# Deformable convolution: the last tile of tokens taken three taps at a time

## The chip, the cores and the metric

The kernel runs on one core of one Trainium2 chip. The metric is the device time of one execution in microseconds (us); lower is better. Times given as a median are of executions without the profiler; the profile is of one further execution.

## The reference

Four layers follow one another on an image batch of 4 x 56 x 56 x 128 floats: a window-attention block, a state-space block, a deformable convolution and another window-attention block, each as `x = x + layer(group_norm(x))`. The change lies in the third layer alone, which the reference computes like this:

```python
offsets = conv(x, offset_w) + offset_b            # 9 taps x (dy, dx) for every pixel
py, px = row + ky + dy, col + kx + dx
y0, x0 = floor(py), floor(px); wy, wx = py - y0, px - x0
val = gather(y0, x0) * (1 - wy) * (1 - wx) + gather(y0, x0 + 1) * (1 - wy) * wx \
    + gather(y0 + 1, x0) * wy * (1 - wx) + gather(y0 + 1, x0 + 1) * wy * wx
out = einsum('bhwkc,kcf->bhwf', val, kernel.reshape(9, C, F)) + bias
...
x = x + L2(group_norm(x))
```

So for every pixel and each of 9 taps, four neighbours of 128 channels are fetched from places that depend on the data, weighted and added, and the nine results are multiplied by a 128 x 128 matrix each and summed.

## The kernel before, in words

The batch of four images is walked one image at a time (`run`), and each image goes through the four layers. `x` holds an image with channels on the 128 partitions and 3136 tokens along the free side. Inside `deform` the kernel writes its own order (`manual_schedule`): each engine executes its instructions in the order in which the Python text issues them, and waits are inserted where data or a buffer demand it.

The tokens are cut in two ways. A **tile** is 112 tokens (`QB`), and there are 28 of them (`NTB`), numbered `t` = 0 to 27. A **chunk** is four tiles, 448 tokens (`CH`), and there are seven (`NCK`), numbered `c` = 0 to 6. Nine taps (`KK`) are handled in three groups of three. Five helpers make up the loop:

- `gather(t)` issues nine indirect DMAs on GpSimd (L1265), one for each tap. They fill the tile `g`, 112 tokens x 9 taps x 512 values; there are four such buffers.
- `weigh(t)` works on VectorE (DVE), three instructions for each group of taps: L1366 multiplies the two far neighbours by their weights into PSUM (`pa`), L1367 multiplies the near ones in place, L1368 adds the two.
- `turn(t)` transposes on TensorE (PE): six instructions for each group of taps (L1379), which also add the two remaining halves, into a PSUM tile `pvt`. ScalarE (ACT) copies each `pvt` into the chunk's tile `vt` (L1380).
- `product(c, i)` multiplies taps 3i to 3i+2 of a whole chunk by the kernel's matrices and accumulates them in the PSUM tile `pdo` (L1387). There is one `pdo` buffer. Each of the three matrix products of a call shows in the trace as two MATMUL records.
- `add(c)` adds `pdo` and the bias to `x` on DVE (L1391), and takes the chunk's statistics for the next group norm (`stats`, L117).

The loop over tiles runs one chunk behind itself: while the tiles 0, 1 and 2 of chunk c are turned, the three products of chunk c-1 are issued, and at tile 3 of chunk c comes `add(c - 1)`. For the last tile, t = 27, this means that DVE gets `weigh(27)` and then `add(5)`, and PE gets `turn(27)`. After the loop come `product(6, 0)`, `product(6, 1)`, `product(6, 2)` and `add(6)`. Then the next layer, `swin("L3")`, begins with its group norm (`gn_mv` L128, `gn_pm` L130), which needs the statistics of all seven chunks, and with the normalized windows `xw` (L235). GpSimd also clears buffers for it, beginning with `ks` (L336).

Of the kernel before, what the change touches and what calls it, by code (L numbers as in the profile page):

```python
# [23 lines left out]
NCK = L // CH  # L24
# [12 lines left out]
NTB = L // QB  # L37
# [12 lines left out]
KK = 9  # L50
# [28 lines left out]
class _Net:  # L79
# [1169 lines left out]
    def deform(self, b, x):  # L1249
# [7 lines left out]
        with tc.tile_pool(name="df", bufs=1) as s1, tc.tile_pool(name="df_ps", bufs=1, space=PSUM) as s1x, tc.manual_schedule():  # L1257
            idx = s1.tile([QB, n2], I32, tag="idx", name="idx")
            patch = {}

            def gather(t):
                patch[t] = s1.tile([QB, KK, 4 * P], F32, tag="g", name="g", bufs=4)
                for k in range(KK):

                    nc.gpsimd.indirect_dma_start(  # L1265
                        out=patch[t][:, k], out_offset=None, in_=tab[:, :],
                        in_offset=bass.IndirectOffsetOnAxis(ap=idx[:, t * KK + k : t * KK + k + 1], axis=0),
                    )
# [4 lines left out]
            with tc.tile_pool(name="dc", bufs=1) as sb, tc.tile_pool(name="dc_ps", bufs=6, space=PSUM) as ps:  # L1273
# [7 lines left out]
                for c in range(NCK):  # L1281
# [3 lines left out]
                    for i in range(nq):  # L1285
                        t = c * nq + i
# [21 lines left out]
                for g in range(2):  # L1308
                    n = min(4, NCK - 4 * g)
                    pf = bank("pf")  # L1310
                    for k in range(KK):
                        ky, kx = k // 3, k % 3
                        for j in range(n):
                            c = 4 * g + j
# [40 lines left out]
            with tc.tile_pool(name="dg", bufs=2) as sb, tc.tile_pool(name="dg_ps", bufs=2, space=PSUM) as ps:  # L1355
                turned, made = {}, {}

                def weigh(t):

                    g = patch[t].rearrange("q k (s c) -> q k s c", s=4)  # L1360
                    wv = wts[2 * t // NTB][:, t % (NTB // 2) * KK : (t % (NTB // 2) + 1) * KK, :, None].to_broadcast([QB, KK, 4, P])
                    for k in range(0, KK, 3):
                        ks = slice(k, k + 3)
                        pa = ps.tile([P, 2, 512], F32, tag="pa", name="pa", bufs=1)
                        far = pa[:QB].rearrange("q a b -> q (a b)")[:, : 6 * P].rearrange("q (k s c) -> q k s c", k=3, s=2)
                        nc.vector.tensor_tensor(far, g[:, ks, 2:, :], wv[:, ks, 2:, :], ALU.mult)  # L1366
                        nc.vector.tensor_tensor(g[:, ks, :2, :], g[:, ks, :2, :], wv[:, ks, :2, :], ALU.mult)  # L1367
                        nc.vector.tensor_tensor(g[:, ks, :2, :], g[:, ks, :2, :], far, ALU.add)  # L1368

                def turn(t):  # L1370
                    c, i = divmod(t, nq)
                    if i == 0:
                        turned[c] = sb.tile([P, KK, CH], F32, tag="vt", name="vt")
                    g = patch.pop(t)
                    for k in range(0, KK, 3):
                        pt = ps.tile([P, 3, QB], F32, tag="tr", name="pvt", bufs=3)
                        for m in range(3):
                            for s in range(2):
                                nc.tensor.matmul(pt[:, m, :], lhsT=g[:, k + m, s * P : (s + 1) * P], rhs=self.ident[:QB, :QB], start=(s == 0), stop=(s == 1), is_transpose=True)  # L1379
                        nc.scalar.copy(turned[c][:, k : k + 3, i * QB : (i + 1) * QB], pt)  # L1380

                def product(c, i):

                    if i == 0:
                        made[c] = ps.tile([P, 512], F32, tag="y", name="pdo", bufs=1)
                    for k in range(3 * i, 3 * i + 3):
                        nc.tensor.matmul(made[c][:, :CH], lhsT=w["kernel"][:, k * P : (k + 1) * P], rhs=turned[c][:, k, :], start=(k == 0), stop=(k == KK - 1))  # L1387

                def add(c):
                    cols = slice(c * CH, (c + 1) * CH)  # L1390
                    nc.vector.scalar_tensor_tensor(x[:, cols], made.pop(c)[:, :CH], w["bias"], x[:, cols], ALU.add, ALU.add)  # L1391
                    self.stats(x, c)


                for t in range(NTB):
                    c, i = divmod(t, nq)
                    if t >= 4:
                        gather(t)
                    weigh(t)
                    if c >= 1 and i == 3:  # L1400
                        add(c - 1)
                    turn(t)
                    if c >= 1 and i < 3:
                        product(c - 1, i)
                for i in range(3):
                    product(NCK - 1, i)
                add(NCK - 1)

    def finish(self, b, x, cols):
# [108 lines left out]
```

## Time and profile before

| | |
|---|---|
| median of 3 executions | 13293.08 us (13291.37 to 13294.18) |
| profiled execution | 13095.61 us |
| its span, first to last instruction | 13093.7 us |
| mean granted TensorE clock | 0.943 of full speed |
| busy share of PE, DVE, ACT, POOL | 89%, 74%, 58%, 76% |
| busy time of L1265 (gathers), all images | 940.8 us, 1008 instructions |
| busy time of L1379 (transposes), all images | 366.7 us, 2016 instructions |

The profiled execution is 197.47 us shorter than the median of the others, and its span leaves 1.91 us of its own time outside. Shares of busy time are averages over four layers in which different engines are the busiest. The trace is one execution; in it a stretch of time is named in us from the start of the span. The four images go through the deformable layer near 2112 to 2434, 5380 to 5704, 8650 to 8970 and 11914 to 12241 us.

### The profile page before, as it was taken

The numbers are of one execution on the slowest core, as the hardware profiler recorded it, in microseconds if no ns is written. First come the engines' busy times: TensorE is split into PE (matmuls) and PEld (weight loads), VectorE is DVE, ScalarE is ACT, GpSimd is POOL, SyncE is SP. The second block draws the span as 40 slices with busy tenths as digits, with TensorE's granted clock in tenths as the row PEclk, the third lists the DMA queues.
The fourth block names the chain that finished last, engine by engine and source line by source line (L and its number), as shares of the span: only waits on it lengthen the run. The fifth ranks groups of instructions, "written<-read, shape, count | busy, mean of one in ns | idle before, by whom it ended". The sixth has DMA issues, their size and how long they took to land. (4 is left out here: it accounts for less than half of the span.)

```text
span 13093.7 us, 216642 instructions
## 1 busy us (share of the span) xinstructions
PE 11654.7 (89%) x84932; PEld 7362.6 (56%) x84932; DVE 9728.0 (74%) x11883; ACT 7560.0 (58%) x19097; POOL 9942.8 (76%) x6852
## 2 busy tenths in 40 slices
PE   8989996799898999679989899967999989996799
PEld 4438884444543888444454388844445438884444
DVE  6659996665665999666566599966656659996665
ACT  5567772356556777235655677723565567772356
POOL 4949995498494999549759499954974949995497
PEclk9999997899999999789999999978999999997899
DMA  1000003200000000420000000042000000004200
GB/s 59 1 14 4 5 4 114 74 1 9 3 1 14 4 5 4 116 72 1 10 2 1 14 5 5 4 120 68 1 11 1 1 14 5 5 4 121 66 1 6
DMA packets 155644, 317.88 MB, mean 24 GB/s; under 512 B 19660, under 2 KB 89344, under 8 KB 154496
## 3 DMA queue, kind: packets, MB, share of 16 engines
q0 software_dynamic: 80640, 231.28, 6.1%
q1 hardware_dynamic: 73696, 71.21, 1.8%
q8 instruction: 672, 11.01, 0.3%
q14 instruction: 348, 2.85, 0.1%
q10 hardware_dynamic: 288, 1.53, 0.0%
HBM read 256.04 MB, written 47.90 MB: 23 GB/s over the span
## 5 line engine op out<-in xcount | busy, mean ns | idle before, releaser
L569 POOL TENSOR_TENSOR es<-es,e 128x896 f32<-128x896 f32 x2016 | 4159.3, 2090 | 133.1 <-ACT e L563 75.1
L363 DVE TENSOR_REDUCE mx<-pm 128x1 f32<-128x512 f32 (+1 forms) x4928 | 3057.9, 671 | 1401.5 <-PE pm L362 787.3
L563 ACT ACTIVATE e<-pst 128x448 f32<-128x448 f32 (+1 forms) x5600 | 2678.4, 544 | 1886.8 <-PE pst L561 1351.4
L1083 DVE TENSOR_TENSOR_SCAN hs<-da,dbu 128x928 f32<-128x928 f32 x1792 | 3633.1, 2070 | 52.2 <-ACT dbu L1076 30.0
L1092 POOL TENSOR_TENSOR hs<-hs,cb 128x896 f32<-128x896 f32 x1792 | 3473.8, 1951 | 25.0 <-ACT carry L1087 20.3
L362 PE MATMUL pm<-ks,qs 32*128 32x512 f32 (+1 forms) x9856 | 2906.1, 633 | 13.3 <-DVE nm L384 7.8
L561 PE MATMUL pst<-qs,ks 32*128 32x448 f32 x11200 | 2684.0, 547 | 0.0
L1101 PE MATMUL yt<-w_C,hs 128*116 128x128 f32 x14336 | 1865.1, 273 | 1.1 <-POOL hs L1092 1.1
L556 PE MATMUL pst<-nm,sel 32*128 32x448 f32 x5600 | 1637.1, 614 | 0.0
L1101 PEld LDWEIGHTS yt<-w_C,hs 128*116 128x116 f32 x14336 | 1571.2, 135 | 2.1 <-POOL hs L1092 2.1
L1065 PE MATMUL dbu<-dgb,ut 112*128 112x224 f32 x7168 | 1258.6, 298 | 268.0 <-DVE hs L1083 267.8
L585 PE MATMUL po<-e,va 128*32 128x448 f32 (+1 forms) x11200 | 1350.8, 551 | 0.0
L362 PEld LDWEIGHTS pm<-ks,qs 32*128 32x128 f32 x9856 | 923.4, 185 | 746.2 <-DVE mx L363 619.3
L1065 PEld LDWEIGHTS dbu<-dgb,ut 112*128 112x128 f32 x7168 | 946.2, 192 | 533.1 <-DVE hs L1083 523.3
L1265 POOL DMA_INDIRECT g<-tab,idx x1008 | 940.8, 933 | 393.6 <-issue 283.1
L1019 ACT ACTIVATE da<-dl,A 128x112 f32<-128x112 f32 x3584 | 1193.9, 382 | 0.1
L561 PEld LDWEIGHTS pst<-qs,ks 32*128 32x128 f32 x11200 | 1096.8, 185 | 100.9 <-issue 12.7
L556 PEld LDWEIGHTS pst<-nm,sel 32*128 32x128 f32 x5600 | 569.9, 184 | 739.9 <-DVE mx L363 387.1
L1379 PE MATMUL pvt<-w_C,g 112*128 112x112 f32 x2016 | 366.7, 338 | 623.4 <-issue 520.4
L1380 ACT COPY vt<-pvt 128x336 f32<-128x336 f32 x336 | 147.2, 438 | 1126.5 <-PE pvt L1379 1126.5
L288 POOL TENSOR_TENSOR pz<-s,m 64x784 f32<-64x784 f32 x128 | 191.8, 1498 | 751.9 <-DVE m L285 520.0
L1087 ACT COPY carry<-hs 128x32 f32<-128x32 f32 x1792 | 397.2, 222 | 624.0 <-DVE hs L1083 615.9
(237 smaller groups left out, 15945.1 us busy)
## 6 DMA issues: line engine op xcount, KB each, us to landing
g<-tab,idx POOLq DMA_INDIRECT x1008, 3.4
tab<-zero SPq DMA_DIRECT2D x4, 3364.0 KB
dl_d<-dl SPq DMA_DIRECT2D x28, 448.0 KB
dl<-dl_d SPq DMA_DIRECT2D x56, 224.0 KB
tab<-gt SPq DMA_DIRECT2D x16, 448.0 KB
out_dram<-x SPq DMA_DIRECT2D x28, 224.0 KB
tab<-gt SPq DMA_DIRECT2D x16, 336.0 KB
x<-in_x_dram SPq DMA_DIRECT2D x21, 224.0 KB
```

Source lines behind the costliest of these rows:

```text
L362: nc.tensor.matmul(pm[:, :m], lhsT=qs[head(h), q.start : q.start + P], rhs=ks[head(h), keys], start=True, stop=True)
L363: nc.vector.tensor_reduce(mx[:, home[i][1], h, kc : kc + 1], pm[:, :m], AX.X, ALU.max)
L556: nc.tensor.matmul(t[:, :CH], lhsT=self.sel[head(h), :], rhs=nm[head(h), part(qc)], start=True, stop=False)
L561: nc.tensor.matmul(t[:, :CH], lhsT=ks[head(h), k * KB : (k + 1) * KB], rhs=qs[head(h), part(qc)], start=False, stop=True)
L563: nc.scalar.activation(e[:nk, j, :], t[:nk, :CH], AF.Exp, scale=SCALE)
L569: nc.gpsimd.tensor_tensor(s, es[g - 1, p][:nk] if k == 1 else s, e[:nk], ALU.add)
L585: nc.tensor.matmul(m["po"][head(h), :CH], lhsT=va[:nk, k, head(h)], rhs=src(h)[:nk], start=(k == 0), stop=(k == NKB - 1))
L1019: nc.scalar.activation(m["da"][:, :, n, 2:], dl(), AF.Exp, scale=A[:, j, n : n + 1])
L1065: nc.tensor.matmul(pu[:, 8 * h : 8 * h + 8, 2 + tb * TB : 2 + (tb + 1) * TB], lhsT=made[g]["ut", 2 * r + tb][:, d, :], rhs=made["r", g // ...
L1083: nc.vector.tensor_tensor_scan(flat(pairs[u // 2][:, d % 2]), flat(made[g]["da"][:, r]), flat(banks.pop(u)), 0.0, ALU.mult, ALU.add)
L1092: nc.gpsimd.tensor_tensor(hs, hs, made["r", g // 2]["cb"][:, :, r * HW : (r + 1) * HW], ALU.mult)
L1101: nc.tensor.matmul(sums[q][:YR, e * P : (e + 1) * P], lhsT=hs[:, n, :], rhs=self.ident, start=(n == 0), stop=(n == NST // 2 - 1), is_trans ...
```

## The change

`weigh` and `turn` take an argument that says which groups of taps they handle. The loop over tiles issues everything for t = 0 to 26 as before, and for t = 27 only the gathers. What is left comes after the loop: first `add(5)`, then for each group of three taps `weigh`, `turn` and, from the second group on, the product of the group before. `product(6, 2)` and `add(6)` are last. The tiles in `patch` are no longer dropped from the dictionary when they are turned.

```diff
-                def weigh(t):
+                def weigh(t, taps=range(0, KK, 3)):
...
-                    for k in range(0, KK, 3):
+                    for k in taps:
...
-                def turn(t):
+                def turn(t, taps=range(0, KK, 3)):
...
-                    g = patch.pop(t)
-                    for k in range(0, KK, 3):
+                    g = patch[t]
+                    for k in taps:
...
-                    weigh(t)
-                    if c >= 1 and i == 3:
-                        add(c - 1)
-                    turn(t)
-                    if c >= 1 and i < 3:
-                        product(c - 1, i)
+                    if t < NTB - 1:
+                        weigh(t)
+                        if c >= 1 and i == 3:
+                            add(c - 1)
+                        turn(t)
+                        if c >= 1 and i < 3:
+                            product(c - 1, i)
+
+                add(NCK - 2)
                 for i in range(3):
-                    product(NCK - 1, i)
+                    weigh(NTB - 1, (3 * i,))
+                    turn(NTB - 1, (3 * i,))
+                    if i >= 1:
+                        product(NCK - 1, i - 1)
+                product(NCK - 1, 2)
                 add(NCK - 1)
```

In the changed program as built, the order of instructions differs at four places, one for each image. On PE the end of the layer was L1379 x18, L1387 x9, and is now L1379 x12, L1387 x3, L1379 x6, L1387 x6. On DVE the pair L1391, L117 of chunk 5 moves ahead of the nine instructions of `weigh(27)`. ACT, GpSimd and the DMA queues have the same instructions in the same order, and every tile has the same address.

## The prediction

> **What bounds the kernel now.** I began with the page. PE is the busiest engine overall, but the change touches one layer, and there the groups point elsewhere: the gathers on GpSimd, while PE's transposes stand idle longer than they work.
>
> ```profile
> PE 11654.7 (89%) x84932; PEld 7362.6 (56%) x84932; DVE 9728.0 (74%) x11883; ACT 7560.0 (58%) x19097; POOL 9942.8 (76%) x6852
> ...
> L1265 POOL DMA_INDIRECT g<-tab,idx x1008 | 940.8, 933 | 393.6 <-issue 283.1
> L1379 PE MATMUL pvt<-w_C,g 112*128 112x112 f32 x2016 | 366.7, 338 | 623.4 <-issue 520.4
> ```
>
> A gather starts every 1.24 us (0.93 busy, 0.30 idle in the timeline), three taps take 3.7 us, and DVE's three instructions for them 2.80 us: DVE waits for the DMA before nearly every group. So in the loop the gathers set the pace; only what follows the last one (issued at 12224.42 in the fourth image) can be shortened. Next I read the timeline of DVE at that end:
>
> ```profile
> 12220.67 0.96 DVE L1366 TENSOR_TENSOR pa<-g,wt 112x768 f32<-112x768 f32 x1 [1.14 <-DMA g<-tab,idx]
> 12221.54 0.95 DVE L1367 TENSOR_TENSOR g<-g,wt 112x768 f32<-112x768 f32 x1
> 12222.52 0.95 DVE L1368 TENSOR_TENSOR g<-g,pa 112x768 f32<-112x768 f32 x1
> 12224.29 0.96 DVE L1366 TENSOR_TENSOR pa<-g,wt 112x768 f32<-112x768 f32 x1 [0.81 <-DMA g<-tab,idx]
> ...
> 12229.72 0.95 DVE L1368 TENSOR_TENSOR g<-g,pa 112x768 f32<-112x768 f32 x1
> 12230.59 0.68 DVE L1391 SCALAR_TENSOR_TENSOR x<-pdo,w_L,x 128x448 f32<-128x448 f32 x1
> 12231.30 0.63 DVE L117 BATCH_NORM_STATS2 gn_st<-x 128x6 f32<-128x448 f32 x1
> ```
>
> The three groups of tile 27 start at 12220.67, 12224.29 and 12227.87 and end at 12230.67. The add of chunk 5, behind them, waits for nothing. The chain of waits shows who is last:
>
> ```profile
> 12220.54 3.82 PE pdo L1387 x6
> 12224.36 0.59 PE pvt L1379 x6
> ...
> 12227.20 1.37 PE pvt L1379 x6
> ...
> 12230.77 1.35 PE pvt L1379 x6
> 12232.13 7.68 PE pdo L1387 x18
> 12239.81 0.02 issue
> 12239.83 0.69 DVE x L1391
> ```
>
> Two facts decide my forecast. The path is the last group's weighing, its transposes, then all 18 MATMUL records of chunk 6, 7.68 us, with DVE idle 7.90 us and the next layer behind it. And the product of chunk 5 (first line) ends at 12224.36, **after** weigh(27) has begun at 12220.67.
>
> Last, the granted clock in stretches (columns: stretch, length, PE busy, clock, DMA share, GB/s):
>
> ```profile
> 12226.00:12227.00 1.00, 0.00 (x0) 0.98 0.71 211
> 12227.00:12228.00 1.00, 0.80 (x5) 0.50 0.06 21
> 12230.40:12233.80 3.40, 3.03 (x9) 0.50 0.00 0
> 12233.80:12237.20 3.40, 3.40 (x10) 1.00 0.00 0
> ```
>
> **What the skill says, and whether the trace agrees.** The Trainium skill, page "TensorE: Matmul & The Clock Gate", section "Part 1: The HAM clock gate", says PE's clock is halved until a free-running window of about 3.4 us has been busy. The trace agrees: only 0.5 and 1.0 occur, and switches fall on a grid of 3.41 us (about 12226.98, 12230.40, 12233.81). A window with PE busy for 1.3 to 1.5 us of 3.4 stayed at half speed (as 12226.98 to 12230.40); one with 3.0 us brought full speed. The threshold between is unseen. The same page, section "Architectural detail", says DVE's queue is strict FIFO and PE pulls only weight loads forward. The timelines agree: no DVE instruction here overtakes a waiting one. So whatever stands behind a waiting add waits too.
>
> **The change part by part**, for the fourth image.
>
> *Add and statistics of chunk 5, moved ahead of weigh(27).* Two DVE instructions, on no queue but DVE's. Before, they cost nothing: they ran under the last transposes. Now the add reaches the head of DVE at about 12219.6, when weigh(26) ends, and needs pdo, finished at 12224.36. That is a **new wait of 4.8 us**, and the nine instructions of weigh(27) stand behind it, though the DMA for the first six taps lands by 12224.29. The add starts at 12224.38, the statistics 0.71 later, the next L1366 0.54 after them (12186.75 to 12187.29 in the timeline): 12225.63, instead of 12220.67. From here all data has landed in time, so groups follow without gaps, 0.87 + 0.98 + 0.87 = 2.72 us apart: 12228.35 and 12231.07. The last ends 2.80 later, at **12233.87 instead of 12230.67**. The DMA wait that hid under the old order is regained, which is why 4.96 us late at the start becomes 3.20 at the end.
>
> *Transposes and products, re-ordered.* Nothing is added to PE. The second group's transposes can start 0.10 after its L1368, at 12231.25. product(6, 0) follows 1.15 later, as before (12230.77 to 12231.92), at 12232.40; its ACT copy is long done. Six records cost 0.745 each at half clock or 0.375 at full clock (starts of the weight loads). The third group's transposes now stand behind this product; their data is ready at 12233.97, so PE, not DVE, is late by then. They take 0.6 at full clock, and the remaining 12 records 12 x 0.375 = 4.5, plus 0.2 for the end of the last one (so calibrated, the old 18 records give 12239.8). ACT's copy of the last group, 0.45 us, lies under product(6, 1).
>
> What is unknown is when full clock comes. The window 12230.40 to 12233.81 would be busy 2.56 of 3.41 us, between the shares seen. (a) If that suffices: 1.41 us of half clock (1.9 records) and 4.1 x 0.375 bring 12235.35; + 0.6 + 4.5 + 0.2 = 12240.65, **0.85 later** than 12239.81. (b) If not, 6 x 0.745 ends at 12236.87, transposes at 12237.6, end at 12242.3, **2.5 later**. I take the middle, 1.6, and keep both.
>
> *Waits.* PE's built list loses one wait on DVE before the products, and the last transposes wait for an earlier group of PE's own instead of an ACT copy. Nearest row: a semaphore event on PE's queue took 0.051 us. So between a gain of 0.05 and a loss of 0.2 (one drained product); I take 0. *patch no longer emptied*: no instruction or address changes; 0.
>
> *The other images* have the same shape: in all four, pdo of chunk 5 ends 6.1 to 6.3 us before the last weighing ends, and the final product ends 15.4 to 15.5 us after pdo of chunk 5. Sum: 4 x 1.6 = 6.4, bounds 4 x 0.85 = 3.4 and 4 x 2.5 = 10, with waits 3.2 to 10.8. Against its own 13095.61 the profiled execution would read 13102. The unprofiled median stood 197 us higher, and I add the same difference to it: 13293.1 + 6 = **13299 us**.
>
> **The rivals.**
>
> *The overlap pays.* Were DVE not held, product(6, 0) would start at 12228.35, run at half clock to 12230.40 and end at 12231.6; transposes and two products bring 12236.9, 2.9 us sooner, 11.6 in all: 13281.5. For it: PE idles 2.26 and 2.22 us between these transposes, and DVE has slack. Against it: the order of adds and weighings in DVE's list and the 12224.36 above. It needs the product of chunk 5 over by 12221, which its transposes (12219.63) do not allow.
>
> *Clock stays low, clearly slower.* The end becomes several bursts with gaps. If neither window after 12230.40 brings full clock, the end is 12232.40 + 4.47 + 1.15 + 8.94 + 0.2 = 12247.2, 7.3 us later, 29 in all: 13322, slower by 0.22%. It decides if PE still shows 0.50 beyond 12237.2. For it: the window before is only 40% busy. Against it: from 12231.25 on PE has no gap[...].
>
> *Clearly faster* needs 6.6 us an image. The last six records plus transposes cannot start before the old 12230.77, so 12230.77 + 0.6 + 2.25 + 0.2 = 12233.8, six us less, is a floor that even a perfect overlap does not pass.
>
> **How the numbers follow.** A measurement of this kernel tells about 0.2%, 26.6 us, from no change. Late add, 3 to 11 us slower: 0.80. Overlap pays: 0.10. Clock stays low: 0.06, on the border, counted as slower. Something unforeseen: 0.04. So faster 0.03, same 0.90, slower 0.07. The range takes the two likeliest cases, 13281.5 to 13304, with some way toward the third: 13281 to 13312.
>
> **What would show it right or wrong.** In the profile after: L1391 of chunk 5 waits 4 to 5 us for PE pdo in each image (before, it waits only for chunk 6: 31.9 us over 4 times); the three L1366 behind it follow 2.72 us apart with no DMA wait; the last weighing ends 3.2 us later; DVE's wait for the last pdo stays between 6.8 and 8.4 us (7.9 before); the end moves by 0.8 to 2.5 us. If L1391 of chunk 5 shows no wait, the step that carries the forecast is wrong.

## The result, and the profile after

The changed kernel took **13338.04 us** (13320.64 to 13348.71, 8 executions) against 13295.36 us (13290.79 to 13303.87, 8 executions) of the kernel before: a ratio of 1.003, interval 1.002 to 1.0039, or 42.7 us more. Repeated on three chips, the difference was 36.9, 37.0 and 34.7 us. The forecast was 6 us.

The page after, three rows of its groups. It shows one of the eight timed executions (13342.97 us). The columns are line, engine, operation, tiles, count; then busy time and mean ns of one; then the idle time just before them and what ended most of it.

```profile
L1265 POOL DMA_INDIRECT g<-tab,idx x1008 | 943.8, 936 | 565.7 <-issue 288.6
...
L1379 PE MATMUL pvt<-w_C,g 112*128 112x112 f32 x2016 | 343.0, 337 | 930.9 <-issue 544.7
...
L1380 ACT COPY vt<-pvt 128x336 f32<-128x336 f32 x336 | 141.2, 441 | 1362.3 <-remote 885.8
```

The gathers work as long as before (943.8 us, 940.8 before), but stand idle 172 us longer than in the profile that the prediction used. And ACT's copies now wait mostly for something that the trace can't name ("remote"). Before, their 1126.5 us of idle time were all put down to PE's transposes:

```profile
L1380 ACT COPY vt<-pvt 128x336 f32<-128x336 f32 x336 | 147.2, 438 | 1126.5 <-PE pvt L1379 1126.5
```

The change does not touch either of them, so this already says that the two profiles differ in more than the change.

DVE's timeline of the kernel after, end of the fourth image (columns: start, length, engine, line, operation; in brackets the idle time and what ended it):

```profile
12460.24 0.95 DVE L1368 TENSOR_TENSOR g<-g,pa 112x768 f32<-112x768 f32 x1
12470.86 0.68 DVE L1391 SCALAR_TENSOR_TENSOR x<-pdo,w_L,x 128x448 f32<-128x448 f32 x1 [9.66 <-PE pdo L1387]
12471.58 0.63 DVE L117 BATCH_NORM_STATS2 gn_st<-x 128x6 f32<-128x448 f32 x1
12472.12 0.94 DVE L1366 TENSOR_TENSOR pa<-g,wt 112x768 f32<-112x768 f32 x1
...
12479.64 0.95 DVE L1368 TENSOR_TENSOR g<-g,pa 112x768 f32<-112x768 f32 x1
12487.80 0.68 DVE L1391 SCALAR_TENSOR_TENSOR x<-pdo,w_L,x 128x448 f32<-128x448 f32 x1 [7.21 <-PE pdo L1387]
```

The new wait is there, and longer than the 4.8 us of the forecast. The add of chunk 5 holds DVE for 9.66 us, and the whole of `weigh(27)` comes after it. The chain of waits of the same stretch shows what follows:

```profile
12468.55 2.27 PE pdo L1387 x6
12470.82 4.19 issue
12475.01 1.37 PE pvt L1379 x6
...
12479.21 3.46 PE pdo L1387 x6
12482.66 0.58 PE pvt L1379 x6
12483.24 4.54 PE pdo L1387 x12
12487.78 0.03 issue
12487.80 0.69 DVE x L1391
```

Chunk 5's product ends at 12470.82, and PE then stands still for 4.19 us while DVE adds and weighs. From the end of chunk 5's product to that of the final product (below: **the tail**) it is 16.9 us here.

One plain fact is needed to read all this. The profile of the kernel before, 13095.61 us, and the timed executions, 13291 to 13304 us, show one program in two conditions, and in these runs each chip showed only one of them. One of the chips used later ran the same kernel in 13099.90 us (13091.41 to 13120.36, 11 executions), four others in 13281 to 13292. The change was measured in the second condition, and forecast from the first. On which chip the profile of the kernel before was taken is not on record.

### The profile page after: what moved, and what is told of

Read it like the earlier page. It is cut to its first block, busy times and chain, and to the rows that moved or that the text cites. A ratio compares the mean times of both kernels' runs of the same rounds, so it can differ in the third digit from the quotient of the medians.

```text
span 13340.9 us, 216634 instructions
## 1 busy us (share of the span) xinstructions
PE 11587.4 (87%) x84932; PEld 7345.5 (55%) x84932; DVE 9743.9 (73%) x11883; ACT 7558.2 (57%) x19097; POOL 9948.8 (75%) x6852
## 5 line engine op out<-in xcount | busy, mean ns | idle before, releaser
L1265 POOL DMA_INDIRECT g<-tab,idx x1008 | 943.8, 936 | 565.7 <-issue 288.6
L1379 PE MATMUL pvt<-w_C,g 112*128 112x112 f32 x2016 | 343.0, 337 | 930.9 <-issue 544.7
L1379 PEld LDWEIGHTS pvt<-w_C,g 112*128 112x128 f32 x2016 | 288.7, 187 | 1015.2 <-issue 621.6
```

## The experiments

The tables here are worked out from the traces. "Late groups" are groups of six transposes whose ACT copy starts over 3 us after their last record ends (of 336). The trace models when a transpose ends, so a late copy can mean a late signal or a transpose that in truth ended late; no run tells the two apart, and "late signals" below stands for both. "Tail" is the mean over the four images. "Gathers" is from the first to the last of an image, and "layer" the sum of the four deformable layers from the group norm of one layer to that of the next.

### The kernel before once more, and the order of DVE alone

`same` is the kernel before, unedited.

> The kernel before, unchanged, for a trace in the condition of the timed executions (13291 to 13304 us, where the profile shown had 13096). Theory A (the difference is made at the end of each image's deformable layer by the add that is held up): the trace has the loop over tiles at the pace of the gathers, as in the profile shown, and the 200 us lie elsewhere. Theory B (the loop over tiles itself runs slower in timed executions, in both kernels, and the change makes it more so): the stretch from the layer's group norm to the next layer's, 351 us in the profile shown and 403 to 409 us in the profile of the changed kernel, measures about 395 us here. Time: ratio 1.000 in both.

`addfirst` moves only the add:

```diff
+                    if t == NTB - 1:
+                        add(c - 1)
                     weigh(t)
-                    if c >= 1 and i == 3:
+                    if c >= 1 and i == 3 and t < NTB - 1:
                         add(c - 1)
```

> The kernel before with one part of the change alone: add(5) ahead of weigh(27); products still after all transposes. Theory A: the last weighing ends 3.2 us later and all of it is on the path, so 4 x 3.2 = 13 us slower, about 13308. Theory B: the hold matters more, because TensorE is further behind in timed executions; as slow as the changed kernel, 13335 or more.

`lateadd` has the changed kernel's order for weighing, turning and multiplying, but puts the add back behind two of the three groups of weighing (the edit is one of the changed kernel):

```diff
-                add(NCK - 2)
                 for i in range(3):
                     weigh(NTB - 1, (3 * i,))
                     turn(NTB - 1, (3 * i,))
+                    if i == 1:
+                        add(NCK - 2)
                     if i >= 1:
                         product(NCK - 1, i - 1)
```

> The changed kernel with add(5) issued after the second group's weighing and transposes, just ahead of product(6, 0). Theory A: DVE is held later and less, the overlap pays: 2.9 us an image sooner than before, about 13284. Theory B, in the form that the hold of the whole weighing costs the 42 us: near before, within 10 us of 13295. Theory C (the order of the products or the number of instructions, not the add, makes the loop slower): still 13335.

`after_again` is the changed kernel, unedited.

> The changed kernel once more beside the others on the same chip: 13338, that is 42 us slower than before, if the difference is one of the kernels; nearer to 13300 if it was one of the chip at that time.

All four ran on one chip, beside the kernel before at 13281.67 us; the table's first and last row are other executions.

| kernel | us | ratio, interval | late groups | gathers, us | tail, us | layer, us |
|---|---|---|---|---|---|---|
| profile that the prediction used | 13095.61 | | 0 | 311 | 15.4 | 1404.8 |
| same | 13282.00 | 0.9999 (0.999 to 1.0007) | 144 | 350 to 354 | 8.5 | 1586.2 |
| addfirst | 13323.26 | 1.0029 (1.0019 to 1.0038) | 149 | 350 to 354 | 19.8 | 1633.7 |
| lateadd | 13284.39 | 1.0003 (0.9995 to 1.0012) | 145 | 350 to 354 | 9.5 | 1591.4 |
| after_again | 13318.60 | 1.0026 (1.0015 to 1.0037) | 145 | 354 | 17.4 | 1609.2 |
| after (first result) | 13338.04 | 1.003 (1.002 to 1.0039) | 145 | 350 to 356 | 17.2 | 1624.0 |

This settles two things. First, the place of the add makes the loss: moved alone, it costs 41.6 us, and with it moved back, the three-taps order costs 2.7 us (5.9 and 7.8 us on two further chips, below), no difference that these runs can tell. Second, the tail gives the size. All that stands ahead of the end of chunk 5's product is the same in these kernels, so a longer tail is time lost. Four images of 17.2 - 8.5 = 8.7 us make 35 us, four of 19.8 - 8.5 = 11.3 make 45, and four of 9.5 - 8.5 = 1.0 make 4. The totals moved by 37 to 43, 42 and 3 us. The layer's sum in a single trace scatters more: against `same` it is 37.8 and 23.0 us longer in the two traces of the changed kernel, 47.5 in `addfirst` and 5.2 in `lateadd`.

The tail is so short in `same` because DVE is early and PE late. DVE's timeline of `same`, fourth image:

```profile
12417.54 0.95 DVE L1368 TENSOR_TENSOR g<-g,pa 112x768 f32<-112x768 f32 x1
12419.15 0.96 DVE L1366 TENSOR_TENSOR pa<-g,wt 112x768 f32<-112x768 f32 x1 [0.66 <-DMA g<-tab,idx]
...
12428.40 0.95 DVE L1368 TENSOR_TENSOR g<-g,pa 112x768 f32<-112x768 f32 x1
12431.12 0.69 DVE L1391 SCALAR_TENSOR_TENSOR x<-pdo,w_L,x 128x448 f32<-128x448 f32 x1 [1.77 <-PE pdo L1387]
12431.84 0.63 DVE L117 BATCH_NORM_STATS2 gn_st<-x 128x6 f32<-128x448 f32 x1
12439.63 0.68 DVE L1391 SCALAR_TENSOR_TENSOR x<-pdo,w_L,x 128x448 f32<-128x448 f32 x1 [7.16 <-PE pdo L1387]
```

`weigh(27)` follows `weigh(26)` after 0.66 us and ends before chunk 5's product does. The add waits for PE even here, 1.77 us, with nothing behind it that matters. After that product only PE's own work is left: 18 transposes and the product of chunk 6, 8.5 us. So the weighing is hidden under PE's backlog, in all four images of this trace. Moving the add ahead of it takes that cover away, as `addfirst` shows in DVE's timeline:

```profile
12468.64 0.96 DVE L1368 TENSOR_TENSOR g<-g,pa 112x768 f32<-112x768 f32 x1
12480.78 0.68 DVE L1391 SCALAR_TENSOR_TENSOR x<-pdo,w_L,x 128x448 f32<-128x448 f32 x1 [11.18 <-PE pdo L1387]
...
12489.56 0.95 DVE L1368 TENSOR_TENSOR g<-g,pa 112x768 f32<-112x768 f32 x1
12499.88 0.69 DVE L1391 SCALAR_TENSOR_TENSOR x<-pdo,w_L,x 128x448 f32<-128x448 f32 x1 [9.37 <-PE pdo L1387]
```

The wait is 11.18 us, and all of 8.5 us of weighing lies between it and PE's transposes. In the changed kernel the tail is 2.6 us shorter than here, since it turns and multiplies the first groups while DVE weighs the later ones: the overlap that the change sets up does exist, and gives back about a quarter (2.6 of 11.3 us) of what the add costs. With the add in third place (`lateadd`, the same view) two of the three groups are weighed before the wait, and only the last group is behind it:

```profile
12423.91 0.95 DVE L1368 TENSOR_TENSOR g<-g,pa 112x768 f32<-112x768 f32 x1
12433.81 0.68 DVE L1391 SCALAR_TENSOR_TENSOR x<-pdo,w_L,x 128x448 f32<-128x448 f32 x1 [8.94 <-PE pdo L1387]
...
12435.07 0.94 DVE L1366 TENSOR_TENSOR pa<-g,wt 112x768 f32<-112x768 f32 x1
...
12443.29 0.68 DVE L1391 SCALAR_TENSOR_TENSOR x<-pdo,w_L,x 128x448 f32<-128x448 f32 x1 [5.43 <-PE pdo L1387]
```

A wait of 8.94 us costs nearly nothing here: when it ends, two groups lie weighed, and PE turns them and begins on chunk 6 while DVE adds and weighs the third. It is what stands behind the waiting instruction that counts, not the wait.

### Why PE has a backlog: its signals and the gathers

The trace of `same` around a gap in the fourth image, PE, ACT and GpSimd in turn:

```profile
12384.32 1.31 PE L1379 MATMUL pvt<-w_C,g 112*128 112x112 f32 x12
12385.86 0.79 PE L1379 MATMUL pvt<-w_C,g 112*128 112x112 f32 x6 [0.23 <-issue]
12408.28 1.38 PE L1379 MATMUL pvt<-w_C,g 112*128 112x112 f32 x6 [21.63 <-issue]
```

```profile
12407.79 0.44 ACT L1380 COPY vt<-pvt 128x336 f32<-128x336 f32 x1 [21.98 <-issue]
12412.75 1.12 ACT L1380 COPY vt<-pvt 128x336 f32<-128x336 f32 x3 [4.52 <-remote]
```

```profile
12406.88 0.93 POOL L1265 DMA_INDIRECT g<-tab,idx  x1 [0.30 <-issue]
12413.06 0.93 POOL L1265 DMA_INDIRECT g<-tab,idx  x1 [5.25 <-remote]
```

These are three groups of transposes, the first ended at 12385.06 and the last at 12386.65. ACT, idle since 12385.81, copies the first at 12407.79, 22.7 us later, and the last at 12413.08, 26.4 us later. PE has three `pvt` buffers and cannot go on without the copies. The signals come through in bursts, here when the gathers pause. In the profile that the prediction used, ACT follows most groups after 0.04 us and every one within 0.2 us.

The trace's own record of semaphores (the counters by which engines and DMAs signal each other) differs in the same way. The gathers should leave 16128 updates in it, 16 for each gather. The profile that the prediction used, `paced64` and `paced128` below have all of them, and the four traces with slow gathers 98 to 99%. All the others have 14 to 34%, `same` 3056. Whether the missing updates were merged or only not recorded can't be told. But it means that "remote" and "issue" name no cause in these traces.

The transfers themselves are not slower: one packet of the gathers takes 163 ns on average in `same` and 158 ns in the profile that the prediction used.

Three questions followed. Is it the bytes of the gathers, their rate, or the few `pvt` buffers?

`half_before` and `half_after` fetch half the bytes, without and with the change. They leave out the second row of neighbours and use the first in its place, so they do not compute the layer:

```diff
-                        out=patch[t][:, k], out_offset=None, in_=tab[:, :],
+                        out=patch[t][:, k, : 2 * P], out_offset=None, in_=tab[:, :],
...
-                        nc.vector.tensor_tensor(far, g[:, ks, 2:, :], wv[:, ks, 2:, :], ALU.mult)
+                        nc.vector.tensor_tensor(far, g[:, ks, :2, :], wv[:, ks, 2:, :], ALU.mult)
```

> The order before, but each gather fetches only the first 256 of 512 values of a token (1 KB instead of 2 KB), and weigh takes both pairs of neighbours from them: the second row of neighbours is left out, all instructions keep their number and size. Theory B1 (TensorE's completion signals come late because of the bytes that the gathers move): the signals of the 336 transposed groups that reach ACT over 3 us late fall from 144 to under 30, the gathers of an image take about 311 us instead of 354, and about 170 us are saved, 13110. Theory B2 (it is the number of gathers or of their descriptors, not the bytes): 144 late groups remain, time within 30 us of 13282.

> The same cut of the gathers in the changed kernel's order. If the late signals are gone, the arithmetic of the prediction holds again: 3 to 11 us slower than half_before. If they remain: 35 to 45 us slower than half_before.

`slow_before` and `slow_after` have GpSimd clear 512 values on each partition after every gather, `paced64` and `paced128` (of the kernel before) 64 and 128 values:

```diff
+            idle = s1.tile([P, 512], F32, tag="idle", name="idle")
...
+                    nc.gpsimd.memset(idle, 0.0)
```

> The order before, all bytes gathered, with a memset of 128x512 on GpSimd after each gather (0.53 us busy in the profile of the kernel before), so that gathers come about every 1.8 to 2.1 us instead of 1.24. Theory B1 and B2 (too many gathers or bytes at a time hold the signals back): late groups fall under 30, the gathers of an image take 450 to 530 us, total slower by 400 to 700 us. If the lateness has nothing to do with the gathers' rate, 100 or more late groups remain.

> The same in the changed kernel's order. TensorE then has time to finish product(5, 2) before the last group of tile 26 is weighed or soon after; by the prediction's arithmetic the hold of DVE costs at most 4.8 us an image and the end moves by under 2.5: within 10 us of slow_before. If the hold costs about 10 us an image whatever TensorE's lag: 40 us slower than slow_before.

> The order before, all bytes gathered, with a short memset (128x64) on GpSimd after each gather: a gather about every 1.3 us (1.24 without it, 1.65 with the memset of 128x512, where no completion signal was late; without it the pauses bring the mean to 1.41). If the signals are late because gathers come faster than something can serve, and 1.3 us is already slow enough: no late groups of 336, the gathers of an image take 320 to 335 us, the layer ends as in the first profile, and 80 to 140 us are saved: 13140 to 13200. If the limit lies between 1.3 and 1.41: late groups remain, 100 or more, and the time is within 20 us of 13281.

> The same with a memset of 128x128: a gather about every 1.35 us. With the signals in time: no late groups, 335 to 350 us for the gathers of an image, 20 to 80 us saved, 13200 to 13260. If they are still late: within 20 us of 13281 or slower.

The last two met the chip on which the kernel before takes 13099.90 us and no group of theirs was late, so `paced64` was run again on another, beside the changed kernel and `lateadd`:

> A gather every 1.27 us. If the kernel before takes about 13100 here: 45 us slower, as measured. If about 13280 and the signals are late because gathers come faster than 1.27 us: no late groups, gathers of an image 319 us instead of 354, about 13145 and so 130 us faster. If 1.27 us is still too fast: 100 or more late groups and within 20 us of before.

> The changed kernel on the chip of this call. If the kernel before takes about 13100 here (TensorE's signals in time, as in the first profile): the prediction's arithmetic, 3 to 11 us slower, and the end of the layer 0.8 to 2.5 us later an image after product(5, 2). If it takes about 13280 (signals late): 35 to 45 us slower again.

> add(5) just ahead of product(6, 0). If the kernel before takes about 13100 here: DVE is not held behind product(5, 2), the overlap pays, 2.9 us an image, 12 us faster (the rival of the prediction, never seen with signals in time). If about 13280: within 10 us of before, as measured.

`tr5` gives PE five `pvt` buffers instead of three, and moves the tile `wt` out of PSUM to make room:

```diff
-            wps = s1x.tile([P, 2, 512], F32, tag="wt", name="wt")
+            wps = s1.tile([P, 2, 512], F32, tag="wt", name="wt")
...
-                        pt = ps.tile([P, 3, QB], F32, tag="tr", name="pvt", bufs=3)
+                        pt = ps.tile([P, 3, QB], F32, tag="tr", name="pvt", bufs=5)
```

> The order before, with five pvt buffers instead of three (the bilinear weights wt move from PSUM to SBUF to make room). If ACT's late copies cost time because TensorE runs out of pvt buffers: the pauses of the gathers shrink and 20 us or more are saved where the signals are late. If the late signals alone set the pace: within 15 us of before. Where they are in time: within 15 us of before.

> The changed kernel on the chip of this call. If the kernel before takes about 13100 here (signals in time): the prediction's arithmetic, 3 to 11 us slower, product(6, 2) ending 16.3 to 17.9 us after product(5, 2) instead of 15.4. If about 13280 (signals late): 35 to 45 us slower, and 17.2 us instead of 8.5.

> add(5) just ahead of product(6, 0). With the signals in time: the overlap pays, product(6, 2) ends about 12.5 us after product(5, 2) instead of 15.4, 12 us faster. With the signals late: 9.5 us instead of 8.5, within 10 us of before.

Lines are grouped by the chip that they share.

| kernel | us | kernel before beside it | ratio, interval | late groups | gathers, us | layer, us |
|---|---|---|---|---|---|---|
| half_before | 13292.71 | 13281.20 | 1.0008 (1.0001 to 1.0014) | 148 | 353 to 356 | 1602.1 |
| half_after | 13323.66 | | 1.0037 (1.0023 to 1.005) | 145 | 355 to 356 | 1620.6 |
| slow_before | 13504.89 | | 1.017 (1.0156 to 1.0184) | 0 | 413 | 1815.5 |
| slow_after | 13521.44 | | 1.0183 (1.0169 to 1.0196) | 0 | 413 | 1812.5 |
| paced64 | 13145.13 | 13099.90 | 1.0031 (1.0019 to 1.0042) | 0 | 319 | 1442.1 |
| paced128 | 13194.70 | | 1.0069 (1.0055 to 1.0083) | 0 | 334 | 1500.5 |
| paced64_c | 13298.02 | 13291.55 | 1.0005 (0.9997 to 1.0013) | 160 | 356 to 359 | 1603.4 |
| after_c | 13328.50 | | 1.003 (1.0017 to 1.0042) | 147 | 355 to 356 | 1618.6 |
| lateadd_c | 13297.43 | | 1.0 (0.9992 to 1.0009) | 155 | 356 | 1589.3 |
| tr5 | 13287.43 | 13285.25 | 1.0002 (0.9993 to 1.001) | 119 | 354 to 355 | 1581.8 |
| after_d | 13319.91 | | 1.0025 (1.0016 to 1.0033) | 146 | 354 | 1611.3 |
| lateadd_d | 13293.07 | | 1.0003 (0.9994 to 1.0011) | 146 | 350 to 354 | 1593.1 |

*Bytes are not it*: half of them left the late groups and the gathers' 355 us as they were, and the change still cost 31 us. The tail says the same: 10.1 us on average in `half_before` and 18.0 in `half_after`, four times the difference being 32 us. *The rate matters*: one gather every 1.65 us (`slow_before`) leaves no group late, on a chip where gathers issued every 1.24 us, with pauses, leave about 145. It is not the clearing as such, since `paced64_c` clears too, if less, and still has 160 late groups. The page of `slow_before2`, the same kernel on a further chip, puts nearly all of ACT's idle time down to PE again:

```profile
L1382 ACT COPY vt<-pvt 128x336 f32<-128x336 f32 x336 | 147.2, 438 | 1537.3 <-PE pvt L1381 1504.2
```

*The buffers are not it either*: with five of them, the layer takes the same time, but GpSimd's timeline (fourth image) looks different:

```profile
12396.40 1.40 POOL L1265 DMA_INDIRECT g<-tab,idx  x1 [0.31 <-issue]
12398.11 0.93 POOL L1265 DMA_INDIRECT g<-tab,idx  x1 [0.30 <-issue]
12399.35 0.93 POOL L1265 DMA_INDIRECT g<-tab,idx  x1 [0.30 <-issue]
12400.59 1.48 POOL L1265 DMA_INDIRECT g<-tab,idx  x1 [0.31 <-issue]
```

The pauses of some 6 us are mostly gone, and instead every third gather takes 1.3 to 1.5 us in place of 0.93. PE's backlog at the end is mostly gone too: the add of chunk 5 waits for nothing in three images, and there the tail is 15.8 to 15.9 us. As chunk 5's product ends earlier, the total is the same, so tails compare only kernels that do the same ahead of it. The changed order with five buffers was not run. The sum is the same: in `same`, `half_before`, `paced64_c` and `tr5` an image's 251 intervals between gathers take 350 to 359 us, 1.39 to 1.43 us each, however the delay is spread. The Trainium skill, page "Perfetto Trace Analysis", section "DMA Instruction — SWDGE (GPSIMD)", says that the profile ends such a DMA when its descriptors are written and not when its data have moved, and that more can be generated than the descriptor buffer holds. The 1.40 us beside 0.93 us fit a full buffer, though no run shows the buffer itself. So I read the 1.4 us as the pace that these chips keep for these gathers, against 1.24 us or less in the profile that the prediction used. That reading is drawn from these kernels alone; no run changed the pace itself, and what makes PE's signals late near it was not found.

The pair with slow gathers is the nearest to what the prediction described, because there DVE waits for data again. Its difference, 16.6 us, was larger than the layer's own (-3.0 us), so it was repeated:

> The paced order before once more: 13505 if the chip has late signals with the kernel before; no late groups; the end of the layer's last product 15.8 us after the last gather, as measured.

> The paced changed order once more. Its layer measured 3 us less than slow_before's in the traces, its total 17 us more. If the 17 us are the execution's or the clock's (the next layer's time varies by several us with TensorE's clock): within 10 us of slow_before2. If they come with the order: 12 to 20 us slower again, and again in the layer after.

Now it was 8.0 us (13514.15, 13499.2 to 13525.84; 13522.13, 13511.64 to 13528.93), with the layer's sum at 1814.7 and 1814.8 us. DVE's timeline of `slow_after2`, fourth image:

```profile
12651.03 0.95 DVE L1370 TENSOR_TENSOR g<-g,pa 112x768 f32<-112x768 f32 x1
12657.66 0.68 DVE L1393 SCALAR_TENSOR_TENSOR x<-pdo,w_L,x 128x448 f32<-128x448 f32 x1 [5.68 <-PE pdo L1389]
12658.38 0.63 DVE L117 BATCH_NORM_STATS2 gn_st<-x 128x6 f32<-128x448 f32 x1
12658.92 0.94 DVE L1368 TENSOR_TENSOR pa<-g,wt 112x768 f32<-112x768 f32 x1
...
12675.86 0.68 DVE L1393 SCALAR_TENSOR_TENSOR x<-pdo,w_L,x 128x448 f32<-128x448 f32 x1 [8.47 <-PE pdo L1389]
```

With signals in time the add holds DVE for 5.68 us, near the 4.8 us of the forecast, and the DMA waits behind it are regained. These waits are longer here, some 2 us for a group where the forecast had about 1. So the layer's last product ends sooner, 14.9 us after the start of the last gather instead of 15.5, where the forecast had it 0.85 to 2.5 us later. The mechanism is the forecast one, but the balance is not the same, so this pair does not measure the forecast itself.

What the whole kernel loses there, 8 to 17 us, lies outside the layer. In the traced executions, which differ by 14.3 and 29.7 us, the layer behind takes 11.1 and 21.1 us more. In the second image of `slow_after2` it takes 4.4 us more than in `slow_before2`, all of it in its first 170 us; near its start PE's clock stays halved for 13.7 us instead of 6.8. Why the clock comes up later there was not found.

## Why the prediction was wrong

*Right in mechanism.* The add of chunk 5 waits in every image, and `weigh(27)` stands behind it. The Trainium skill, page "TensorE: Matmul & The Clock Gate", section "Architectural detail", says that DVE's queue is strict FIFO, and the trace agrees: L1366 comes only after the held add and its statistics, at 12472.12. The groups behind it start without a DMA wait, 2.83 us apart (2.72 forecast). DVE waits 7.0 to 8.0 us for the last `pdo` (6.8 to 8.4 forecast). The last twelve records take 4.54 us (4.5 forecast at full clock), so the clock does come up: the rival in which it stays low is out.

*Right for the state after.* By the prediction's own numbers the tail after would be 12240.65 - 12224.36 = 16.3 us in case (a), and 12242.3 - 12224.36 = 17.9 us in case (b). It measured 17.2 us on average, single images 16.8 to 17.8. This is no luck: once the add has waited, all data has landed, and the work that follows is the same however late the add was. One reading was wrong, though with little effect: "The threshold between is unseen". Cut into windows of 3.41 us, the trace of the kernel before has 49 at half clock in which PE is busy for 50 to 80%, and each is followed by another at half clock. That speaks for case (b). Nor is a busy window enough: of 141 at half clock with PE busy for over 95%, 13 are followed by half clock.

*Wrong for the state before.* The failed step is the one sentence "The unprofiled median stood 197 us higher, and I add the same difference to it". It treats the 197 us as a constant beside the change. Nearly all of them lie in the changed layer: it takes 1586.2 - 1404.8 = 181 us more in the trace of `same`, of 192 us between the two traced executions, while each of the other three layers agrees within 6.3 us over all images. There the gathers and PE keep other times. So the tail before is 8.5 us and not 15.4, and the term of the sum is 8.7 us an image instead of 1.6. What made the loss small, a DMA wait to be regained on the path and the weighing as the last thing there, holds where PE keeps up, as in the profiled execution. In `same` DVE still waits for the DMA before the groups of tile 27 (0.66, 0.88 and 0.91 us in the fourth image), but PE's backlog hides them. The wait itself, sized at 4.8 us from when DVE and PE reach the add, was 7.9 to 15.1 us.

*The rivals.* "The overlap pays" named the condition on which it fails, chunk 5's product not over when `weigh(26)` is, and it failed on that: the product ended 7.9 to 15.1 us after it. "Clock stays low, clearly slower" came nearest to the size (29 us), for a reason that the trace rules out. The question that was not asked is which layer holds the 197 us.

*Open.* The changed kernel never met a chip whose signals are in time, so the forecast for that condition, 6 us, was not tried itself. The next layer takes 3398 to 3418 us for the four images in four traces of the changed kernel (mean 3405) and 3397 to 3415 us in three of `lateadd`. In four traces with the order before and late signals (`same`, `half_before`, `paced64_c`, `tr5`) it takes 3391 to 3405 us (mean 3397). So a few us may be lost there too, but the ranges overlap, and no run tells whether any of the few us between 35 and the measured 35 to 43 is due to it. What makes the signals late, and why on some chips only, is open.

## What to carry to other kernels

When a profiled execution and the timed ones differ by far more than the change could bring, find the stretch in which they differ before carrying a result from one to the other; if it is the stretch that is changed, the profile is not the baseline. An instruction that waits for a slow engine costs what is queued behind it: with all of the last tile's weighing behind it the add cost 42 us, with a third of it 3 to 8, which is within the noise. Work that is hidden by another engine's backlog should be priced with the backlog taken away, and with a larger one.

## What the runs showed of the hardware

One kernel, with nothing edited, took 13099.90 us on one chip and 13281 to 13292 us on four others. On three of the latter, traced without slowing the gathers, a stream of gathers of 112 rows each went at 1.39 to 1.43 us per gather whether it carried 2 KB or 1 KB per row, and beside it ACT's copies started up to 42 us after the trace's end of PE's transposes, with 119 to 160 of 336 groups over 3 us; at 1.65 us per gather none was over 0.2 us late. In the traces with late signals, the record of semaphores held 14 to 34% of the gathers' updates, in the others 98% or more.
